# Loading six of eight heads' Wq and Wk in 32-wide blocks, and letting each pair's score weights follow its own product

## The chip, the cores and the metric

The kernel runs on one NeuronCore of a Trainium2 chip. The core has a matrix engine (TensorE, PE in the profile, with its weight loads listed as PEld), a vector engine (VectorE, DVE), an activation engine (ScalarE, ACT), a general engine (GpSimd, POOL) and a queue engine (SyncE, SP) that here issues all the DMAs. Sixteen DMA engines carry the transfers. Each engine works through its own list of instructions in order and waits on semaphores for the others. The metric is device time in microseconds (us), the median of several executions.

## The reference, cut to what matters

Cross attention with a layer norm: 16 batches, 256 query rows of 256 numbers, 77 context rows of 192 numbers, 8 heads of 256. All is float32.

```
Q = x @ Wq            # x (16, 256, 256), Wq (256, 8*256)
K = c @ Wk            # c (16, 77, 192),  Wk (192, 8*256)
V = c @ Wv            # Wv (192, 8*256)
score = Q K^T / 16, per head;  score = -inf where mask == 0
attn  = softmax(score)
out   = concat_heads(attn V) @ Wo + x          # Wo (8*256, 256)
y     = (out - mean) * rsqrt(var + 1e-5) * gamma + beta
```

## The kernel before, in words

The kernel never forms Q, K or V. Per head h it forms G_h = Wk_h Wq_h^T / 16, a matrix of 192 x 256, and U_h = Wv_h Wo_h, once for all batches. A batch's scores are then x (G_h^T c^T), and its output is attn (c U_h). In the code G is split by its 192 rows: `gA` holds the first 128 rows for 8 heads, `gB` the last 64, two heads above each other. `cA` and `cB` hold the transposed context in the same two parts. `prepare_a` (L183) multiplies G with the context of four batches (308 columns): its `part_A` issues the products with gA and cA, four 32-column matmuls beside each other in the array (L202), its `part_B` those with gB and cB, eight beside each other (L216). The results, named a, are what a query tile is multiplied with in `scores` (L319).

The matmuls run in float32; each appears in the trace as two records of weight load and matmul.

Before the loop over batches stands a preparation, about the first 54 us, which the change touches. In order of TensorE's list (L812 to L881):

- `keep_busy` (L657): transposes of the identity whose result is not used, 14 before the first weights and 4 more after the first k transposes.
- `turn_k`, `turn_q`, `turn_k_last`: Wq and Wk need their columns on the partitions for the product G. Heads 0, 1, 4 and 5 are loaded by rows (`wq_nat`, `wk_nat`, `wk_last`) and turned by TensorE, 128 x 128 at a time, into PSUM; ACT and DVE copy the results to `qT` and `kT`.
- `g_of(e)` (L777): G's first 128 rows for two of those heads, scaled by ACT into gA. `rest_of_g(u)` (L791): the last 64 rows, scaled by DVE into gB. Between them `turn_c` turns the first context rows.
- `turn_blk(e)` (L698): heads 2, 3, 6 and 7 are loaded in pieces of 32 rows by 32 columns laid so (`wk_blk`, `wq_blk`) that a DVE transposition of 32 x 32 blocks finishes the turn, into `kT_blk` and `qT_blk`. In this form a pair of heads lies on the two halves of the partitions, and a matmul contracts over 64 rows, two at once in the array.
- `a_of_places((0, 1))`: part_A and part_B for the four turned heads, eight PSUM banks; the copies out alternate between ACT and DVE (`evacuate`).
- `of_pair` (L735) and `rest_of_pairs` (L747): G of the four other heads, then `a_of_places((2, 3))` for them.
- `turn_v` (L727, DVE), then `pu` and `pw`: U of all heads by the same two functions, with Wv and Wo; `turn_rest` turns the remaining context rows on DVE.
- The mask: one 616 KB load broadcasts it to all partitions; DVE turns zeros into large negative numbers (L856) and reduces to find not-a-number entries (L867), POOL folds these in (L868 to L870).
- `transpose_x`: DVE finishes the turn of x for four batches (eight tiles of 128 rows). `prepare_last` (`pr`, L278 and L290) is a product with U for the last 13 context rows of every batch. L290 reads uB, of which half is written by copies on POOL (L865).

Then the loop: for each batch, scores on TensorE, `shift` on DVE, exponentials on ACT, `weigh` on DVE and POOL, `turn` on DVE, and the product with the values. Most batches take `seven`, seven block products in place of eight, fed by sums (`sums`, `differences`) that POOL forms.

The order on each engine is that of the program text; nothing reorders it. SP issues DMAs in order and keeps at most eight in flight: each issue waits until the DMA eight places before it has landed. PSUM is a ring of eight banks under one tag. Tiles of one tag in a pool share a buffer: before, the second half of Wo (`wo_of[1]`) shares that of wq_nat.

Of the kernel before, what the change touches and what calls it, by code (L numbers as in the profile page):

```python
# [15 lines left out]
P = 128  # L16
# [6 lines left out]

# [3 lines left out]
def kernel(  # L54
# [126 lines left out]


    def prepare_a(g, places, B_first=False):  # L183


        if 0 in places:
            a_of[g] = in_two("a", [P, 2, GB, H, S2], g)
        parts = [
            (u + NF * i, dc) for u in places for dc in range(2) for i in range(2)
        ]  # L190
        batches = slice(g * GB, (g + 1) * GB)
        banks = []

        def cols(dc, i):
            return slice((2 * i + dc) * BK, (2 * i + dc + 1) * BK)

        def part_A():
            if not B_first:
                banks.extend(ring_of(parts))
            for (h, dc), o in zip(parts, banks):  # L200
                for i in range(NM):
                    nc.tensor.matmul(  # L202
                        flat(o[i * BK : (i + 1) * BK]),
                        gA[:, h, cols(dc, i)],
                        flat(cA[:, batches, :]),
                        start=not B_first,
                        stop=B_first,
                    )

        def part_B():  # L210
            if B_first:
                banks.extend(ring_of(parts))
            for j in range(0, len(parts), 2):
                for i in range(NM):
                    for k, (h, dc) in enumerate(parts[j : j + 2]):
                        nc.tensor.matmul(  # L216
                            flat(banks[j + k][i * BK : (i + 1) * BK]),
                            gB[half(k), h % NF, cols(dc, i)],
                            flat(cB[half(k), batches, :]),
                            start=B_first,  # L220
                            stop=not B_first,
                        )

        def ring_of(parts):
            return [
                ps_mm.tile([P, GB, S2], F32, tag="mm", name=f"pa_{g}_{h}_{dc}") for h, dc in parts
            ]

        def copies():
            return [(a_of[g][:, dc, :, h, :], o) for (h, dc), o in zip(parts, banks)]  # L230

        return part_A, part_B, copies
# [347 lines left out]

    early = ctx.enter_context(tc.tile_pool(name="early", bufs=1))
    pools[0] = turned = early
    with tc.tile_pool(name="wonce", bufs=1) as wp:
# [4 lines left out]
        wq_nat = wp.tile([P, 2, 2, 2 * D], F32, tag="w128", name="wq_nat")  # L588
        wk_nat = wp.tile([P, 2, 2 * D], F32, tag="wk", name="wk_nat")
        wk_last = wp.tile([P, 2 * D], F32, tag="wl", name="wk_last")  # L590


        wq_blk = wp.tile([P, 2, DI // BK, P], F32, tag="wqb", name="wq_blk")
        wk_blk = wp.tile([P, 2, NL, P], F32, tag="wkb", name="wk_blk")
        wq_blocks = wq.rearrange("(m r) (a i f) -> a i r m f", r=BK, a=NF, i=NM)
        wk_blocks = wk.rearrange("(m r) (a i f) -> a i r m f", r=BK, a=NF, i=NM)
        wq_rows = wq.rearrange("(t p) (e f) -> e p t f", p=P, e=2)
        wk_rows = wk[:P].rearrange("p (e f) -> e p f", e=2)
        wk_ends = wk[P:].rearrange("r (e f) -> (r e) f", e=2)
# [26 lines left out]
        nc.sync.dma_start(wk_nat[:, 0], wk_rows[0][:, : 2 * D])  # L626
        nc.sync.dma_start(wq_nat[:, 0], wq_rows[0][:, :, : 2 * D])
        nc.sync.dma_start(wk_nat[:, 1], wk_rows[1][:, : 2 * D])
        nc.sync.dma_start(wq_nat[:, 1], wq_rows[1][:, :, : 2 * D])
        nc.sync.dma_start(wk_last, wk_ends[:, : 2 * D])  # L630
        nc.sync.dma_start(c_sb, c_rows[:, :first, :])
        for e in range(2):
            load_blocks(wk_blk[:, e], wk_blocks[2 * e + 1])
            load_blocks(wq_blk[:, e], wq_blocks[2 * e + 1])
# [5 lines left out]
            wp.tile([P, 2, 4, DI], F32, tag=tag, name=f"wo_{i}") for i, tag in enumerate(("wo", "w128"))  # L640
# [5 lines left out]
        for a in range(NF):  # L646
            nc.sync.dma_start(wo_of[a // 2][:, a % 2], wo_rows[a])
        load_rest()
        nc.sync.dma_start(
            bias_f.bitcast(I32), mask.rearrange("b k -> (b k)").partition_broadcast(P)  # L650
        )
        load_xT(0)
# [8 lines left out]
        keep_busy(14)  # L661


        qT = const.tile([P, 2, 2, 2, DI], F32, tag="xg0", name="qT")
        kT = const.tile([P, 2, 2, 2, DL], F32, tag="xg2", name="kT")
        qT_blk = const.tile([P, 2, 4, DI], F32, tag="xg1", name="qT_blk")
        kT_blk = const.tile([P, 2, 4, DL], F32, tag="xg3", name="kT_blk")

        def turn_chunks(of, name):

            pt = ps_mm.tile([P, 4, P], F32, tag="mm", name=f"pt_{name}")
            for i, chunk in enumerate(of):
                nc.tensor.transpose(pt[:, i], chunk, ident)
            return pt

        def turn_q(e, u):
            chunks = [
                wq_nat[:, e, t, u * D + dc * P : u * D + (dc + 1) * P]
                for dc in range(2) for t in range(2)
            ]  # L680
            pt = turn_chunks(chunks, f"q_{e}_{u}")
            evacuate(flat(qT[:, e, u]), flat(pt))

        def turn_k(e):
            pt = turn_chunks([wk_nat[:, e, n * P : (n + 1) * P] for n in range(4)], f"k_{e}")
            evacuate(
                kT[:, e].rearrange("p u n l -> p (u n) l")[:, :, :P], pt
            )

        def turn_k_last():  # L690
            pt = turn_chunks([wk_last[:, n * P : (n + 1) * P] for n in range(4)], "kl")
            for e in range(2):
                evacuate(
                    kT[:, e].rearrange("p u n l -> p (u n) l")[:, :, P:],
                    pt.rearrange("p n (r e) -> p e n r", e=2)[:, e],
                )

        def turn_blk(e):  # L698
            for blk, of in ((wk_blk, kT_blk), (wq_blk, qT_blk)):
                nc.vector.transpose(  # L700
                    of[:, e].rearrange("p n (m r) -> p m n r", r=BK),
                    blk[:, e].rearrange("p m (n c) -> p m n c", c=BK),
# [29 lines left out]

# [32 lines left out]
        def wq_part(a, e, n):  # L765
            return qT_blk[half(e), a, n]

        def wk_part(a, e, n):
            return kT_blk[half(e), a, n]

# [6 lines left out]
        def g_of(e):  # L777

            pg = ps_mm.tile([P, 2, DI], F32, tag="mm", name=f"pg_{e}")
            for u in range(2):  # L780
                for dc in range(2):
                    nc.tensor.matmul(  # L782
                        pg[:, u],
                        kT[:, e, u, dc, :P],
                        qT[:, e, u, dc],
                        start=(dc == 0),
                        stop=(dc == 1),
                    )
            nc.scalar.mul(gA[:, NF * e : NF * e + 2], pg, D ** -0.5)

        def rest_of_g(u):  # L791

            ph = ps_mm.tile([P, DI], F32, tag="mm", name=f"ph_{u}")
            for dc in range(2):
                for e in range(2):
                    nc.tensor.matmul(
                        ph[half(e)],
                        kT[:, e, u, dc, P:],
                        qT[:, e, u, dc],
# [3 lines left out]
            nc.vector.tensor_scalar(gB[:, u], ph, D ** -0.5, None, ALU.mult)  # L803

        def a_of_places(places):
            part_A, part_B, copies = prepare_a(0, places)
            part_A()
            part_B()
            for dst, src in copies():
                evacuate(dst, src)  # L810

        turn_k(0)  # L812
        keep_busy(4)
        turn_q(0, 0)
        turn_q(0, 1)
        g_of(0)
        turn_k(1)
        turn_q(1, 0)
        turn_q(1, 1)
# [3 lines left out]
        rest_of_g(0)  # L823
        rest_of_g(1)
        turn_blk(0)
        turn_blk(1)
        a_of_places((0, 1))
        pg = two_banks("pgb", 0)
        for e in range(2):
            of_pair(pg, e, wk_part, wq_part)  # L830
        for i in range(2):
            nc.scalar.mul(gA.rearrange("p (e u) d -> p u e d", e=2)[:, 2 + i], pg[i], D ** -0.5)
        for i, ph in enumerate(rest_of_pairs(0, (0, 1), wk_part, wq_part, "phb")):
            nc.vector.tensor_scalar(gB[:, 2 + i, :], ph, D ** -0.5, None, ALU.mult)
        for a in range(3):
            turn_v(a)
# [3 lines left out]
        a_of_places((2, 3))  # L840
# [15 lines left out]
        nc.vector.tensor_scalar(bias_f, bias_f.bitcast(I32), 0.0, -MASKED, ALU.is_equal, ALU.mult)  # L856
# [9 lines left out]
        nan = wp.tile([P, B, 1], F32, tag="nan", name="nan")  # L866
        nc.vector.tensor_reduce(nan[:, :, 0], bias, AX.X, ALU.max)  # L867
        nc.gpsimd.tensor_tensor(nan, nan, nan, ALU.mult)  # L868
        nc.gpsimd.tensor_tensor(nan, nan, nan, ALU.subtract)
        nc.gpsimd.tensor_tensor(bias, bias, nan.to_broadcast([P, B, S2]), ALU.add)  # L870
# [5 lines left out]
        for j in range(0, GT, 2):  # L876
# [9 lines left out]


# [4 lines left out]
    for b in range(-1, B - 1):  # L892
# [29 lines left out]
        if old and b < B - 2:  # L922
            spread(old[0], old[-1] + 1)
        for _, _, copies in work:
# [100 lines left out]
```

## Time and profile before

| what | value |
|---|---|
| time, median of 3 runs (lowest, highest) | 276.06 us (275.85, 276.31) |
| span of the profiled execution, first to last instruction | 274.2 us |
| the runs' median less that span | 1.9 us |
| TensorE busy (records) | 267.6 us (6012) |
| DVE, POOL, ACT busy | 210.1, 161.0, 132.3 us |
| HBM read and written | 17.57 MB and 4.19 MB |
| first matmul on loaded Wq (pt_q) | at 6.46 us |
| pu begins | at 34.5 us |
| L290 begins | at 48.2 us |
| scores of batch 0 begin | at 54.3 us |
| seven products of batch 0 begin | at 74.6 us |

The profile is of one execution on the chip. It gives no other time for that execution than its span; what a run's time holds beyond the span is taken from the medians. Busy time counts an engine's instructions, but a busy TensorE need not be at its peak, as the ends of matmuls are modelled. The chain is followed back from the last instruction, at each step to what released it, so it tells which engine's time would shorten the run. A wait in brackets behind a group names what ended the idle time before it.

### The profile page before, as it was taken

To read this page: it belongs to the slowest core of one execution; us is meant where nothing else is said; L and a number is where in the kernel's file an instruction comes from. 1 tells how busy PE (TensorE), PEld (TensorE's weight loads), DVE (VectorE), ACT (ScalarE), POOL (GpSimd) and SP (SyncE) were. 2 spreads that over 40 slices of the span, in tenths; PEclk is the share of its full clock that TensorE was granted. 3 is DMA by queue.
4 is the path that set the end of the run, shared out by engine and by line. 5 is a ranking of instruction groups with operands and counts; after the bars stand their busy time and mean duration, and the time that the engine had idled before them with its cause. 6 is when DMAs were issued, how large, how long until landed. Compare 5 with 4: busy or idle time off the path is not lost.

```text
span 274.2 us, 13451 instructions
## 1 busy us (share of the span) xinstructions
PE 267.6 (98%) x6012; PEld 190.4 (69%) x6012; DVE 210.1 (77%) x407; ACT 132.3 (48%) x420; POOL 161.0 (59%) x222
## 2 busy tenths in 40 slices
PE   7999999999999999999999999999999999999993
PEld 7857486777494949595958586867777776584652
DVE  0364966697749898979789797878788978889875
ACT  2314112354818282737464646455464644727652
POOL 1000004939677878787868777777787537255754
PEclk9999999999999999999999999999999999999998
DMA  6996999920000131410230405000505060110102
GB/s 179 245 204 167 338 148 175 239 41 5 4 4 2 57 65 44 154 45 4 59 63 22 100 14 182 28 18 10 116 5 117 2 196 2 41 41 4 60 23 79
DMA packets 40458, 22.63 MB, mean 83 GB/s; under 512 B 23424, under 2 KB 38864, under 8 KB 40400
## 3 DMA queue, kind: packets, MB, share of 16 engines
q1 hardware_dynamic: 40400, 21.77, 32.0%
q8 instruction: 47, 0.77, 1.3%
q14 instruction: 11, 0.09, 0.1%
HBM read 17.57 MB, written 4.19 MB: 79 GB/s over the span
## 4 chain that ended last, share of the span: by engine, by line
PE 96%; DMA 2%; DVE 1%; issue 0%; SPq 0%; DVEq 0%
PE ps L319 25%; PE pa L202 12%; PE pv L244 10%; PE po L452 9%; PE pm L452 8%; PE po L384 7%; PE pa L216 6%; PE pv L255 6%; PE pu L739 3%; PE pr L278 2%; DMA wq_nat<-in_L_xattn_Wq_dram 2%; PE pg L782 1%; PE pgb L739 1%; PE pw L753 1%; PE pr L290 1%; PE po L400 1%
## 5 line engine op out<-in xcount | busy, mean ns | idle before, releaser
L348 ACT ACTIVATE e<-s,top 128x77 f32<-128x77 f32 x256 | 67.1, 346 | 68.0 <-DVE top L341 65.4
L362 POOL TENSOR_TENSOR p<-e,rden 128x512 f32<-128x512 f32 x64 | 47.3, 760 | 42.3 <-DVE rden L356 29.8
L319 PE MATMUL ps<-a,xT 128*32 128x154 f32 x2048 | 70.0, 294 | 0.0
L319 PEld LDWEIGHTS ps<-a,xT 128*32 128x32 f32 x2048 | 66.1, 110 | 1.7 <-issue 0.8
L334 DVE TENSOR_TENSOR s<-ps,bias 128x308 f32<-128x308 f32 x64 | 30.3, 475 | 17.7 <-PE ps L319 17.6
L202 PE MATMUL pa<-cA,gA 128*32 128x308 f32 x512 | 35.8, 423 | 0.0
L202 PEld LDWEIGHTS pa<-cA,gA 128*32 128x32 f32 x512 | 16.4, 110 | 20.9 <-issue 8.0
L485 POOL TENSOR_TENSOR xg<-xg,m 128x256 f32<-128x256 f32 x33 | 24.1, 731 | 11.4 <-DVE xg L499 9.6
L244 PE MATMUL pv<-uA,cA 128*32 128x512 f32 x256 | 30.4, 592 | 0.0
L354 DVE TENSOR_REDUCE den<-e 128x8 f32<-128x616 f32 x32 | 24.7, 773 | 4.4 <-ACT e L348 4.4
L372 DVE STREAM_TRANSPOSE pT<-p 128x640 f32<-128x640 f32 x32 | 25.4, 816 | 1.8 <-POOL p L362 1.8
L341 DVE TENSOR_REDUCE top<-s 128x8 f32<-128x616 f32 x32 | 25.4, 795 | 1.1
L926 ACT COPY vw<-pv 128x512 f32<-128x512 f32 x32 | 17.1, 586 | 8.8 <-PE pv L255 8.8
L415 POOL TENSOR_TENSOR ts<-vw 128x768 f32<-128x768 f32 x11 | 20.3, 1843 | 0.0
L568 DVE SCALAR_TENSOR_TENSOR xg<-xg,rstd,bet 128x256 f32<-128x256 f32 x24 | 18.7, 780 | 1.8
L216 PE MATMUL pa<-cB,gB 64*32 64x308 f32 x512 | 19.5, 420 | 0.0
L216 PEld LDWEIGHTS pa<-cB,gB 64*32 64x32 f32 x512 | 9.7, 107 | 11.3 <-issue 7.6
L255 PE MATMUL pv<-uB,cB 64*32 64x512 f32 x256 | 17.4, 601 | 0.0
L384 PE MATMUL po<-vw,pT 128*32 128x256 f32 x288 | 17.3, 380 | 0.0
L926 ACT COPY a<-pa 128x308 f32<-128x308 f32 x48 | 16.8, 455 | 0.0
L499 DVE TENSOR_TENSOR xg<-po,xg 128x256 f32<-128x256 f32 x31 | 11.7, 412 | 6.1 <-PE po L452 5.6
L452 PE MATMUL po<-vr,pT 128*32 128x128 f32 x352 | 15.7, 273 | 0.0
(121 smaller groups left out, 386.3 us busy)
## 6 DMA issues: line engine op xcount, KB each, us to landing
xg<-in_x_dram SPq DMA_DIRECT2D x4, 1024.0 KB, 6.3
xT<-in_x_dram SPq DMA_DIRECT2D x24, 128.0 KB, 3.5
out_dram<-xg SPq DMA_DIRECT2D x11, 256.0 KB, 2.5
wo<-in_L_xattn_Wo_dram SPq DMA_DIRECT2D x4, 512.0 KB, 5.1
wvT<-in_L_xattn_Wv_dram SPq DMA_DIRECT2D x16, 96.0 KB, 3.4
out_dram<-xg SPq DMA_DIRECT2D x10, 128.0 KB, 1.7
wq_nat<-in_L_xattn_Wq_dram SPq DMA_DIRECT2D x2, 512.0 KB, 6.3
wq_blk<-in_L_xattn_Wq_dram SPq DMA_DIRECT2D x8, 128.0 KB, 5.2
```

The costliest lines, as they stand in the source:

```text
L202: nc.tensor.matmul(flat(o[i * BK : (i + 1) * BK]), gA[:, h, cols(dc, i)], flat(cA[:, batches, :]), start=not B_first, stop=B_first,)
L216: nc.tensor.matmul(flat(banks[j + k][i * BK : (i + 1) * BK]), gB[half(k), h % NF, cols(dc, i)], flat(cB[half(k), batches, :]), start=B_fir ...
L244: nc.tensor.matmul(pv[k][i * BK : (i + 1) * BK], cA[:, b, k * BK : (k + 1) * BK], uA[:, parts, :, i], start=True, stop=False,)
L255: nc.tensor.matmul(pv[k][i * BK : (i + 1) * BK], cB[half(k), b, k * BK : (k + 1) * BK], uB[half(k), parts, :, i], start=False, stop=True,)
L319: nc.tensor.matmul(ps[m // 2][i * BK : (i + 1) * BK, m % 2 * 2 * S2 : (m % 2 + 1) * 2 * S2], xT_of[g][:, j * NM + m, dc], flat(a_of[g][:, ...
L334: nc.vector.tensor_tensor(s[:, a * H // 2 : (a + 1) * H // 2], ps[a][:, : H // 2 * S2].rearrange("p (h k) -> p h k", k=S2), bias[:, b, :]. ...
L341: nc.vector.tensor_reduce(top, s, AX.X, ALU.max, negate=True)
L348: nc.scalar.activation(e[:, h], s[:, h], AF.Exp, bias=top[:, h : h + 1])
L362: nc.gpsimd.tensor_tensor(part, e_mh[:, :, :, keys], rden_mh.unsqueeze(3).to_broadcast(list(part.shape)), ALU.mult,)
L384: nc.tensor.matmul(po[i * BK : (i + 1) * BK], pT[:, n, i], vw_of[b][:, 2 - n // 2 * 2 : 4 - n // 2 * 2, n % 2, :] if n < NF else vr[:, b, ...
L452: nc.tensor.matmul(out[i * BK : (i + 1) * BK], weight[:, i], moving, start=(n == 0), stop=(n == len(terms) - 1),)
L926: nc.scalar.copy(dst, src)
```

## The change

- Only heads 0 and 1 are loaded by rows and turned by TensorE: 14 transposes in place of 28. `wq_nat` comes in two loads of 256 KB, one per head, `wk_last` in two of 64 KB. Each head's q copies are split between DVE and ACT.
- Heads 2 to 7 are loaded in blocks, as three pairs; a pair's `turn_blk` runs one pair ahead.
- After each pair's G (`g_of_pair`, `rest_of_g_of_pair`) its part_A and part_B follow at once (`a_of_pair`), on four banks, with all four copies on ACT. Pairs are now heads 2a and 2a + 1. In `rest_of_g_of_pair` the product is cut into two halves of 128 columns, so that each half of the banks holds one, and DVE writes gB in four pieces.
- `keep_busy` has 12 transposes at the start and none later.
- The mask is loaded and prepared in two parts, batches 0 to 3 and 4 to 15 (`load_bias`, `bias_of`); the second part's work on DVE and POOL moves into the first pass of the loop, behind the weighing. x for the first four batches is loaded in two halves; the second half's DVE turns move to the same place.
- `wo_of[1]` now shares the buffer of wq_blk.

```diff
@@ loads
-        wq_blk = wp.tile([P, 2, DI // BK, P], F32, tag="wqb", name="wq_blk")
-        wk_blk = wp.tile([P, 2, NL, P], F32, tag="wkb", name="wk_blk")
+        wq_blk = wp.tile([P, NF - 1, DI // BK, P], F32, tag="wqb", name="wq_blk")
+        wk_blk = wp.tile([P, NF - 1, NL, P], F32, tag="wkb", name="wk_blk")
...
-        nc.sync.dma_start(wk_nat[:, 0], wk_rows[0][:, : 2 * D])
-        nc.sync.dma_start(wq_nat[:, 0], wq_rows[0][:, :, : 2 * D])
-        nc.sync.dma_start(wk_nat[:, 1], wk_rows[1][:, : 2 * D])
-        nc.sync.dma_start(wq_nat[:, 1], wq_rows[1][:, :, : 2 * D])
-        nc.sync.dma_start(wk_last, wk_ends[:, : 2 * D])
+        nc.sync.dma_start(wk_nat, wk[:P, : 2 * D])
+        for e in range(2):
+            nc.sync.dma_start(wq_nat[:, :, e * D : (e + 1) * D], wq_rows[:, :, e * D : (e + 1) * D])
+        for e in range(2):
+            nc.sync.dma_start(wk_last[half(e)], wk_ends[:, e])
         nc.sync.dma_start(c_sb, c_rows[:, :first, :])
-        for e in range(2):
-            load_blocks(wk_blk[:, e], wk_blocks[2 * e + 1])
-            load_blocks(wq_blk[:, e], wq_blocks[2 * e + 1])
+        for a in range(1, NF):
+            load_blocks(wk_blk[:, a - 1], wk_blocks[a])
+            load_blocks(wq_blk[:, a - 1], wq_blocks[a])
...
-            wp.tile([P, 2, 4, DI], F32, tag=tag, name=f"wo_{i}") for i, tag in enumerate(("wo", "w128"))
+            wp.tile([P, 2, 4, DI], F32, tag=tag, name=f"wo_{i}") for i, tag in enumerate(("wo", "wqb"))
...
-        nc.sync.dma_start(
-            bias_f.bitcast(I32), mask.rearrange("b k -> (b k)").partition_broadcast(P)
-        )
-        load_xT(0)
+        load_bias(0, GB)
+        load_xT(0, 0, GT // 2)
+        load_xT(0, GT // 2, GT)
+        load_bias(GB, B)
...
-        keep_busy(14)
+        keep_busy(12)
@@ the products
+        def turn_q(e):
+            for dc, copy in enumerate((nc.vector.tensor_copy, nc.scalar.copy)):
+                pt = ps_mm.tile([P, 2, P], F32, tag="mm", name=f"pt_q_{e}_{dc}")
+                for t in range(2):
+                    nc.tensor.transpose(
+                        pt[:, t], wq_nat[:, t, e * D + dc * P : e * D + (dc + 1) * P], ident
+                    )
+                copy(qT[:, e, dc], flat(pt))
...
+        def g_of_pair(a):
+            banks = [ps_mm.tile([P, DI], F32, tag="mm", name=f"pgb_{a}_{e}") for e in range(2)]
+            for n in range(4):
+                for e in range(2):
+                    nc.tensor.matmul(
+                        banks[e],
+                        kT_blk[a][half(e), n, :P],
+                        qT_blk[a][half(e), n],
...
+            for e, o in enumerate(banks):
+                nc.scalar.mul(gA[:, 2 * a + e], o, D ** -0.5)
+
+        def rest_of_g_of_pair(a):
+            banks = [ps_mm.tile([P, P], F32, tag="mm", name=f"phb_{a}_{e}") for e in range(2)]
+            for n in range(4):
+                for i in range(2):
+                    for e in range(2):
+                        nc.tensor.matmul(
+                            banks[e][half(i)],
+                            kT_blk[a][half(e), n, P:],
+                            qT_blk[a][half(e), n, i * P : (i + 1) * P],
...
+            for e, o in enumerate(banks):
+                for i in range(2):
+                    nc.vector.tensor_scalar(
+                        gB[half(e), a, i * P : (i + 1) * P], o[half(i)], D ** -0.5, None, ALU.mult
+                    )
+
+        def a_of_pair(a):
+            part_A, part_B, copies = prepare_a(0, (a,))
+            part_A()
+            part_B()
+            for dst, src in copies():
+                nc.scalar.copy(dst, src)
@@ their order
-        turn_k(0)
-        keep_busy(4)
-        turn_q(0, 0)
-        turn_q(0, 1)
-        g_of(0)
-        turn_k(1)
-        turn_q(1, 0)
-        turn_q(1, 1)
-        turn_k_last()
-        g_of(1)
-        turn_c()
-        rest_of_g(0)
-        rest_of_g(1)
-        turn_blk(0)
-        turn_blk(1)
-        a_of_places((0, 1))
...
-        a_of_places((2, 3))
+        turn_k()
+        turn_q(0)
+        g_of(0)
+        turn_q(1)
+        turn_k_last()
+        g_of(1)
+        turn_c()
+        rest_of_g()
+        turn_blk(1)
+        a_of_pair(0)
+        for a in range(1, NF):
+            g_of_pair(a)
+            rest_of_g_of_pair(a)
+            if a + 1 < NF:
+                turn_blk(a + 1)
+            else:
+                for i in range(3):
+                    turn_v(i)
+            a_of_pair(a)
@@ the mask and x
+    def bias_of(lo, hi):
+        part = bias[:, lo:hi]
+        part_f = bias_f[:, lo * S2 : hi * S2]
+        nc.vector.tensor_scalar(part_f, part_f.bitcast(I32), 0.0, -MASKED, ALU.is_equal, ALU.mult)
+        nan = st.tile([P, hi - lo, 1], F32, tag="nan", name=f"nan_{lo}", bufs=1)
+        nc.vector.tensor_reduce(nan[:, :, 0], part, AX.X, ALU.max)
+        nc.gpsimd.tensor_tensor(nan, nan, nan, ALU.mult)
+        nc.gpsimd.tensor_tensor(nan, nan, nan, ALU.subtract)
+        nc.gpsimd.tensor_tensor(part, part, nan.to_broadcast([P, hi - lo, S2]), ALU.add)
...
-        nc.vector.tensor_scalar(bias_f, bias_f.bitcast(I32), 0.0, -MASKED, ALU.is_equal, ALU.mult)
+        bias_of(0, GB)
...
-        nan = wp.tile([P, B, 1], F32, tag="nan", name="nan")
-        nc.vector.tensor_reduce(nan[:, :, 0], bias, AX.X, ALU.max)
-        nc.gpsimd.tensor_tensor(nan, nan, nan, ALU.mult)
-        nc.gpsimd.tensor_tensor(nan, nan, nan, ALU.subtract)
-        nc.gpsimd.tensor_tensor(bias, bias, nan.to_broadcast([P, B, S2]), ALU.add)
...
-        for j in range(0, GT, 2):
+        for j in range(0, GT // 2, 2):
             transpose_x(0, j)
@@ the loop over batches, behind exponential and weigh
+        if b < 0:
+            bias_of(GB, B)
+            for j in range(GT // 2, GT, 2):
+                transpose_x(0, j)
```

## The prediction

> **What bounds the kernel now.** I read the page first (busy time, then the chain by engine), then the chain in order of time, then the timeline of the first 56 us, where the change lies. The page:
>
> ```profile
> span 274.2 us, 13451 instructions
> ...
> PE 267.6 (98%) x6012; PEld 190.4 (69%) x6012; DVE 210.1 (77%) x407; ACT 132.3 (48%) x420; POOL 161.0 (59%) x222
> ...
> PE 96%; DMA 2%; DVE 1%; issue 0%; SPq 0%; DVEq 0%
> ```
>
> TensorE (PE) holds 96% of the chain, so another engine matters only where it makes PE wait. The chain in order of time (start, length, what):
>
> ```profile
> 1.16 5.25 DMA wq_nat<-in_L_xattn_Wq_dram
> ...
> 7.99 1.97 PE pg L782 x8
> ...
> 14.08 1.88 PE ph L796 x16
> 15.96 4.28 PE pa L202 x64
> 20.24 2.23 PE pa L216 x64
> 22.48 3.65 PE pgb L739 x32
> 26.13 1.89 PE phb L753 x32
> ...
> 34.53 7.11 PE pu L739 x64
> ```
>
> The only long item besides PE is the first wq_nat load, landing at 6.41. From there PE runs almost gapless to pu at 34.5 and on to the end: a DMA's arrival, then a sum of PE blocks. On the timeline two later waits come close to PE:
>
> ```profile
> 44.73 0.80 DVE L856 TENSOR_SCALAR bias<-bias 128x1232 f32<-128x1232 int32 x1 [2.32 <-DMA bias<-in_mask_BxS_if_dram]
> ...
> 48.15 2.83 PEld L290 LDWEIGHTS pr<-cRB,uB 64*64 64x64 f32 x64 [0.30 <-POOL uB L865]
> ```
>
> DVE is stopped 2.3 us by the mask; its uB copies queue behind that, POOL's uB copies behind those, and PE at L290 is released by POOL, still without a hole in the chain.
>
> **What the Trainium skill says.** "TensorE: Matmul & The Clock Gate", section "What's actually happening": PE's clock starts at half rate and goes full after about 3.4 us of sustained activity. The trace agrees: 14 idle transposes from 1.36 take 3.25 us (0.21 each at steady rate), eight at 6.46 take 1.10 (0.11 each). "TensorEngine Tiling (Array Packing)", "Key Properties": changing the tiling mode drains the array. The trace agrees: each block here costs 0.14 to 0.19 us beyond its streaming (below).
>
> **The change, part by part.** Times are of the profiled execution, against its 274.2 us span; the runs' median is 276.06, 1.9 us lie around the span, and I carry that over.
>
> Start. wk_nat (256 KB) lands 3.1 us after issue, at 3.84; the 512 KB wq_nat at 6.41, 2.6 us later. The new first wq_nat is 256 KB in pieces of 1 KB instead of 2: half of 2.6 is 1.3, 1.6 if short pieces cost more. It lands at 5.15 to 5.45; I take 5.35, a gain of 1.1 us. PE itself is free at about 4.8 (12 idle and 4 k transposes at 0.21).
>
> Early blocks. Transposes of q, k and kl fall from 28 to 14; the 14 removed are 14 x 0.11 = 1.5 us less PE. From 5.35: four q transposes, still at the slow clock (0.9), their halves copied by DVE and ACT side by side (0.42, from the 128x256 copy of kT), so g_of(0) starts at 6.7. It is half of L782's x8, so 0.9; then 6 transposes 0.7; a wait of 0.3 for the qT halves; g_of(1) 0.9; turn_c 0.6 as before; rest_of_g half of L796 plus switch, 1.0. A of pair 0 starts at 11.2; before, pa started at 15.96 after twice the heads.
>
> Longer or shorter blocks. Each matmul leaves two records. Four pa matmuls run beside each other, one such group per 0.26 us, and 16 groups make 4.14 of L202's 4.28; the rest, 0.14, is the block's own start. The same split: L216 8 x 0.26 + 0.16; pgb 16 x 0.216 + 0.19; phb 8 x 0.216 + 0.16. A pair now has four blocks: g_of_pair 8 x 0.216 + 0.19 = 1.92; rest_of_g_of_pair 16 matmuls of 128 columns, four at once, 8 groups; A 8 x 0.26 + 0.14 = 2.2; B 4 x 0.26 + 0.16 = 1.2. The 64x64 weight with 128 columns has no row. The nearest, pm L452 with 128 columns, has 64 records in 1.89 us, 0.11 per group of four without starts: 0.88 + 0.16 = 1.03. From below it can't go under that stream time, 0.88; from above, if weight loads of 0.13 each limited it, 8 x 0.13 + 0.16 = 1.2. I take 1.03. So a pair is 6.4 us, three are 19.1, pair 0's A and B are 3.4: pu starts at 11.2 + 3.4 + 19.1 = 33.7, against 34.5. Arithmetic is unchanged; 1.5 us of transposes are saved and about 1.3 us returned, since the A, B and G blocks number 14 instead of 6, at 0.16 each.
>
> Does DVE keep up? Per pair it does four gB evictions of 64x128 behind phb (no row: 0.2 each as half of L834's 0.42 at 128x256, up to 0.42; I take 0.23), then turn_blk of the next pair, 0.95 + 1.22 (L700). With hand-overs 3.3 us, while PE needs 3.4 for that pair's A and B. It just hides; at 0.42 each PE would stand 0.7 us at each of two pairs. ACT has four a copies (0.52 apart) and two gA (0.37 each), 2.8 us of 6.4: hidden.
>
> Do the loads keep up? Bytes ahead of wv are the same. In before the second half's blocks landed by 21.2 (DVE L700 waited 2.0 for them), a pair's 896 KB of blocks in 4.2 to 5.2 us. Natural rows now end near 8, so pair 1 lands at 12.3 to 13.0, pair 2 near 17, pair 3 near 22. They are wanted at 13.2 (the qT turn must start then for PE at 14.6), 19.7 and 26. Pair 1 is the tight one, up to 0.5 us. On SP the eight more block issues keep the pace of the landings they wait for. The wo rows of pairs 2 and 3 now share wq_blk's buffer and wait for turn_blk(3), near 27.3; before, they were issued from 27.6. No loss, unless pair 3 slips; behind them on SP stand the context, the mask and x.
>
> pu to prepare_last. The turns of wv (1.6 each, three then one) start at 31.3 and end at 37.6, each before its pu block. PE reaches L290 at 47.4. Its releaser changes: the mask for four batches is a quarter of 616 KB and no longer the late item; now it is cB's last block of context rows. That landed at 40.5; then turn 1.1, uA copy 0.7, bias_of's two DVE steps (0.25 + 0.4, from 0.80 and 1.44 at four times the width), POOL's nan steps and sum (0.3 + 0.3 + 0.6), which now stand ahead of the uB copies, and six of those at 0.46. PE is released at 47.2, if the context lands no later than before. It hides by 0.2. The half of turned x (512 KB instead of 1 MB ahead of scores) lands near 46, wanted at 53: hidden. The split costs SP five more issues (one mask, four x, about 0.45 each, 2.3 us) ahead of load_x(0), gamma and beta; those rows landed at 53 to 55 and are first read by the batch 0 sums near 78: hidden by more than 20 us.
>
> Moved into the first pass: bias_of(4, 16) and two x turns put 0.6 + 1.1 + 1.3 us on DVE after the weighing and 2.3 on POOL before differences. Behind them turn(0), turn(1) and the next shift come 2.1 to 2.5 us later, and sums end 18.1 us after that pass's scores began. seven(0) on PE starts 20.3 after (74.6 against 54.25). Hidden by 2.2 us; without that cover the price would be the excess.
>
> Sum: 1.1 (earlier start) less 0.3 in the early blocks is 0.8, and 0.1 from L290's small release delay that goes: 274.2 - 0.9 = 273.3 span, 275.2 for the runs.
>
> **The rivals.** (1) The gain is lost to the loads at L290 or the pairs: no change. For it: the block loads move in 512 byte pieces, DMA is 0.9 to 1.2 busy in most slices from 2 to 20 us, and three DVE and POOL steps now lie between the context and PE. If the context lands d later, PE gets 1.1 - d; with d of 0.6 to 1.6 the result lies within 0.5 of before. I take d = 0.9: 275.9. Against: the same bytes lead, and SP's issue, not DMA, was the limit from 22 to 26 (busy share 0.4 to 0.6).
> (2) More gain. If the first wq_nat lands at 4.8, where PE is free, and loads and DVE never bite, another 0.5 to 0.7: 274.5. For it: of the 16 DMA engines the first had delivered its share of the 512 KB at 4.45, only the last at 6.41.
> (3) Slower: PE's clock. The second keep_busy (four transposes) is gone, and PE stands idle from 4.8 until wq_nat lands. If that hole, with the one before g_of(0), spoils the activity window that made the clock full near 6.2, one more window of 3.4 us passes at half rate, 1.7 us of lost work: 275.2 + 1.7 = 276.9. It decides from a hole of unknown length; the forecast's is 0.5 us in 3.4. Against: the window stays some 80% busy.
> That the change doesn't do what it says I hold unlikely: the orders of the engines show the blocks where the diff puts them.
>
> **How the numbers follow.** Forecast 275.2 with chance 0.50 (own range 274.8 to 275.5: start time and a few tenths at pair 1); rival 1 0.25; rival 2 0.10; rival 3 0.15. 0.2% is 0.55 us, about what a measurement of this kernel can tell from no change, so faster means below 275.5. That is nearly all of the forecast and rival 2, 0.58; same is most of rival 1 and the forecast's edge, 0.27; slower is rival 3, 0.15. The range from 274.5 to 276.6 holds the forecast, rival 1, the near half of rival 2 and the edge of rival 3; it takes in DVE at 0.42 per eviction (+1.4) and the weight loads (+0.5).
>
> **What would show it.** Start: pt_q released by wq_nat near 5.3. Clock: eight-transpose spacing 0.11 by g_of(0). Blocks: phb 128 columns at 1.0 per pair, pa A 2.2, B 1.2. DVE: no PE wait named L685 at the second and third pair. pu at 33.7. L290's successor released by POOL near 47.4. If pu starts early but scores do not, rival 1 holds; if the early blocks themselves are long, rival 3. The forecast is wrong if PE waits for a turn_blk by more than 0.3 per pair, or if the seven-product block of batch 0 waits for sums.

## The result and the profile after

After: 276.63 us, median of 21 runs; before, beside it on the same chip: 276.13 us. The ratio is 1.0015 with a 95% interval of 1.0003 to 1.0027. Measured again beside each other (below) the two kernels gave 276.46 against 275.89 us, 1.0021 (1.0008 to 1.0035). So the change costs about half a microsecond, where I had forecast a gain of 0.9: the time came out 1.4 us above the forecast of 275.2 and just past the upper end of its range, 276.6. The profiled execution has a span of 274.8 us, 0.6 us above that of before.

Where the front gained is seen on TensorE's timeline of after (start and length in us, engine and line, operation, out<-in, matmul tile, shapes, count of records; in brackets an idle time and what ended it):

```profile
4.91 0.70 PE L664 MATMUL pt_q<-ident,wq_nat 128*128 128x128 f32 x4
...
13.89 2.00 PE L783 MATMUL pgb<-qT,kT 64*128 64x256 f32 x16
15.82 1.10 PE L799 MATMUL phb<-qT,kT 64*64 64x128 f32 x32
...
20.42 2.00 PE L783 MATMUL pgb<-qT,kT 64*128 64x256 f32 x16
...
33.31 7.18 PE L723 MATMUL pu<-wo,wv_turned 64*128 64x256 f32 x64
...
46.99 0.57 PE L260 MATMUL pr<-cRB,uB 64*64 64x208 f32 x4
```

The first transposes of Wq start at 4.91 us instead of 6.46, the product of Wv and Wo (pu) at 33.31 instead of 34.47, and `pr`'s second part (L260, L290 of before) at 46.99 instead of 48.15: 1.16 us gained, more than the 0.8 forecast, and still in hand at 47 us. The next step takes it away. The chain of waits for this stretch, in order of time (start, length, what), first before's, then after's:

```profile
41.64 3.61 PE pw L753 x64
45.26 2.96 PE pr L278 x32
48.22 3.14 PE pr L290 x62
51.36 2.96 PE pr L278 x32
54.32 1.69 PE ps L319 x45
```

```profile
31.61 4.21 SPq L593
35.86 1.06 SPq L593
36.97 1.49 SPq L593
38.50 3.19 DMA cB<-in_ctx_dram
41.79 1.11 DVE cB L601
42.93 0.69 DVE uA L123
43.65 0.48 DVE bias L555
44.16 0.48 DVE nan L557
...
45.28 0.71 POOL bias L560
46.04 0.39 POOL uB L865
...
48.32 0.41 POOL uB L865
48.77 3.03 PE pr L260 x60
51.80 2.96 PE pr L248 x32
54.77 4.32 PE ps L289 x128
```

In before, this stretch of the chain was TensorE alone. Now it comes through the landing of the context's last block (41.69 us; 40.48 in before), goes over VectorE's (DVE) turn and one copy of uA, the two DVE steps of the mask, POOL's three steps of the mask and six of POOL's eight copies of uB, and reaches TensorE at 48.77. Four records of L260 went ahead at 46.99; the other 60 take 3.03 us, as long as the whole block takes without a wait (3.04 in the first experiment), so the block is 48.77 - 46.99 = 1.78 us late. The scores start at 54.70 us instead of 54.25. Ahead of the landing the chain is SyncE itself, issuing the context's loads (SPq L593): one issue takes 4.21 us, with six loads in flight at its start and three at its end, fewer than the eight that the kernel allows. Before has such a long issue too (3.81 us at 29.68); what holds SyncE there no run shows.

From there on the work of the two kernels runs alike: in the traces of both kernels and of all variants below, each of the 16 batches' scores starts within 0.01 us of the same distance from the first (199.42 or 199.43 us from the first to the last), seven(0) starts 20.34 us after the scores in both, and DVE's last instruction ends 217.4 us after them in both. So the work moved into the loop's first pass is hidden.

One difference is left at the very end. From the landing of the last output to the end of the span 0.84 us pass in before and 1.03 us in after. SyncE's list closes with one wait on a semaphore in before and with four in after, some 0.06 us each. Every kernel of this document with mask and x in one piece takes 0.83 to 0.85 us there, every one with the split 1.00 to 1.10. So of the 0.64 us between the two spans, 0.45 are the later scores and 0.19 this closing, for which my prediction had nothing.

### The profile page after: what moved, and what is told of

It reads as the page before. It is cut to its first block, busy times and chain, and to the rows that moved or that the text cites. A ratio compares the mean times of both kernels' runs of the same rounds, so it can differ in the third digit from the quotient of the medians.

```text
span 274.8 us, 13574 instructions
## 1 busy us (share of the span) xinstructions
PE 266.8 (97%) x6056; PEld 188.2 (68%) x6056; DVE 210.5 (77%) x411; ACT 134.0 (49%) x431; POOL 161.9 (59%) x225
## 4 chain that ended last, share of the span: by engine, by line
PE 81%; SPq 8%; DMA 6%; DVE 2%; POOL 1%; issue 1%; DVEq 0%; POOLq 0%
PE ps L289 24%; PE pv L214 10%; PE pa L172 9%; PE po L422 9%; PE pm L422 8%; PE po L354 7%; PE pv L225 6%; DMA wq_blk<-in_L_xattn_Wq_dram 5%; PE pa L186 5%; SPq L593 3%; SPq L582 3%; DMA cB<-in_ctx_dram 1%; PE pr L260 1%; PE pr L248 1%; POOL uB L865 1%
## 5 line engine op out<-in xcount | busy, mean ns | idle before, releaser
L385 POOL TENSOR_TENSOR ts<-vw 128x768 f32<-128x768 f32 x11 | 20.2, 1838 | 0.0
```

## The experiments

**Theories.** In the trace of after two things stand between TensorE and its uB: the context's landing, 1.2 us later than in before (D), and the mask's steps, put ahead of the uB copies on DVE and POOL (P). As my prediction had it, either alone would leave the wait hidden or nearly so; so the question is which of them carries it. "Theory J" below is that both are needed, "theory M" that the split mask's steps alone are what costs.

**The mask's steps behind the copies.**

```diff
-        bias_of(0, GB)
         for j in range(NF // 2):
...
+        bias_of(0, GB)
         for u in (uA, uB):
```

> Theory P (the gain is lost in POOL's queue: the mask's steps stand ahead of the eight copies of uB): the copies can start when cRB is copied, at 44.4 us in the trace of after, and eight of them at 0.45 us end at 48.0 instead of 48.7; the second half of the sixteen-batch product's remainder starts 0.7 us earlier, and so does all that follows: 0.5 to 0.8 us below after, about 0.3 us below before. Theory D (the gain is lost only because the context's remainder lands 1.2 us later): VectorE and POOL still start from the same landing at 41.7 us, and the time stays that of after within 0.2 us.

275.45 us, ratio to before 0.9981 (0.9969 to 0.9993): 1.0 to 1.2 us below after's two medians. POOL and TensorE on this kernel's timeline:

```profile
43.23 0.36 POOL L603 COPY cRB<-cB 128x208 f32<-128x208 f32 x1
43.65 3.67 POOL L864 COPY uB<-uB 64x256 f32<-64x256 f32 x8
```

```profile
47.02 3.04 PE L260 MATMUL pr<-cRB,uB 64*64 64x208 f32 x64
49.99 3.03 PE L248 MATMUL pr<-cRA,uA 128*64 128x208 f32 x32
```

The copies follow the context's own copies at once, L260 runs through, the scores start at 52.95. P is right in kind; its size was too small because it waited for all eight copies, where six are enough. The context landed at 40.84 us here, 0.85 earlier than in the first trace of after, so the medians and the pair below are the better measure. D alone falls.

**After again, and the mask's addition twice.** Both measured beside each other:

```diff
-        nc.gpsimd.tensor_tensor(part, part, nan.to_broadcast([P, hi - lo, S2]), ALU.add)
+        for _ in range(2 if lo == 0 else 1):
+            nc.gpsimd.tensor_tensor(part, part, nan.to_broadcast([P, hi - lo, S2]), ALU.add)
```

> The kernel after, unchanged, as a second look beside the runs of this comparison. Theory J: the context lands between 41 and 42 us again, at least 0.5 us later than the 40.1 to 40.5 of the kernel before, the remainder waits 0.9 to 1.4 us for POOL, and the time is 0.2 to 0.6 us above before. Rival X (the late landing was an accident of one execution): the context lands by 40.6, no wait, 0.9 us below before.

> After, with POOL's addition of the first four batches' mask made twice, 0.7 us more ahead of the copies of uB. Theory P/J: POOL is what the remainder waits for, and the wait grows by the whole 0.7 us: 0.6 to 0.8 us above after. Theory D alone (the wait is for the context): POOL has room, less than 0.2 us above after.

After again: 276.46 us. With the addition twice: 277.41 us, ratio to before 1.0062 (1.0036 to 1.0088), 0.95 us above after and a little more than expected. The timelines, after again first, then the doubled addition:

```profile
44.51 0.70 POOL L560 TENSOR_TENSOR bias<-bias,nan 128x308 f32<-128x308 f32 x1
45.27 3.58 POOL L865 COPY uB<-uB 64x256 f32<-64x256 f32 x8
```

```profile
47.07 0.57 PE L260 MATMUL pr<-cRB,uB 64*64 64x208 f32 x4
47.99 3.03 PE L260 MATMUL pr<-cRB,uB 64*64 64x208 f32 x60 [0.36 <-POOL uB L865]
```

```profile
44.68 1.47 POOL L561 TENSOR_TENSOR bias<-bias,nan 128x308 f32<-128x308 f32 x2
46.22 3.57 POOL L866 COPY uB<-uB 64x256 f32<-64x256 f32 x8
```

```profile
47.26 0.57 PE L260 MATMUL pr<-cRB,uB 64*64 64x208 f32 x4
48.93 3.03 PE L260 MATMUL pr<-cRB,uB 64*64 64x208 f32 x60 [1.10 <-POOL uB L866]
```

The context landed at 40.93 us in both (in the trace of after above it was 41.69), and L260 is 0.92 and 1.67 us late: 0.75 more for 0.77 more of addition. POOL is what TensorE waits for, one for one. After again and the kernel with the steps behind are the cleanest pair: the context's last copy on POOL (cRB) begins at 43.24 and 43.23 us, the uB copies at 45.27 and 43.65, the scores at 53.92 and 52.95; the medians differ by 1.01 us. The expectation of a landing after 41 us missed: it came at 40.93, and L260 still waited. Between the two traces of after the landing differs by 0.76 us and the start of the scores by 0.78: the landing, too, passes through one for one.

**Earlier context, by leaving a load out.** The last quarter of Wo is not loaded; heads 6 and 7 take the rows of heads 4 and 5. Once as after, once with the mask's steps behind.

```diff
-        for a in range(NF):
+        for a in range(NF - 1):
             nc.sync.dma_start(wo_of[a // 2][:, a % 2], wo_rows[a])
...
         def wo_part(a, e, n):
+            a = min(a, NF - 2)
             return wo_of[a // 2][half(e), a % 2, n, :]
```

> The last quarter of Wo isn't loaded; heads 6 and 7 use the rows of heads 4 and 5, so this quarter's share of the result is left out. All loads behind it move up by what it took, about 1.3 us. Theory D: the context lands at about 40.4 us, VectorE's turning, POOL's copies and the remainder's start move up by the same 1.2 us, and the time is 1.0 to 1.3 us below after. Theory P: the mask's steps still stand ahead of the copies; VectorE's bias steps end at 43.4, POOL's at 44.7, eight copies of 0.45 us end at 48.3: only 0.3 to 0.5 us below after.

> As in the run before, the last quarter of Wo is left out; and the mask's steps stand behind the copies of uB. Theory P with D as its second half: POOL is free at 43.2 us, eight copies end at 46.8, just before TensorE wants them (46.99): no wait is left and the time is 1.6 to 1.8 us below after. Theory D alone: the same 1.0 to 1.3 us as with the quarter left out and the mask's steps where they are.

275.75 us, 0.9998 (0.9983 to 1.0012), and 275.22 us, 0.9975 (0.9966 to 0.9984). In the first, the context landed at 40.17 us, the sixth copy of uB ended at 47.19 and L260 ran without a stop from 47.48, with the mask's steps where they were. But pair 1's blocks came late there (TensorE stood 0.37 us for their turn, pu began at 33.79): at after's 46.99 L260 would still have waited 0.2 us. The time lies between the two expectations. With both, 0.2 us less than with the steps behind alone, within the intervals: 1.2 to 1.4 us below after, less than P had given it (1.6 to 1.8) and about what D had (1.0 to 1.3).

What these runs show is P, with D adding to it; J is not shown. In three traces with the mask's steps ahead (both of after and this one) the sixth copy ended 7.01 or 7.02 us after the landing. At before's landings, 40.10 to 41.07 us in three traces, that would be 47.1 to 48.1, still later than the 46.99 at which L260 was reached (an estimate from these figures). An earlier landing so makes the wait smaller; putting the steps behind took it away.

**POOL's copies halved.** All of Wo again, the steps behind, and ScalarE (ACT) writes its half of uB to both places.

```diff
                     engine(here, pw[half(i)].rearrange("p (n c) -> p n c", c=BK))
-                    nc.gpsimd.tensor_copy(there, here)
+                    if i:
+                        nc.gpsimd.tensor_copy(there, here)
+                    else:
+                        engine(there, pw[half(i)].rearrange("p (n c) -> p n c", c=BK))
```

> All of Wo is loaded again. The mask's steps stand behind the copies of uB, and ScalarE writes its halves of uB to both places out of PSUM, so that POOL has four copies instead of eight. Theory P: POOL's four end at about 46.2 us, VectorE's at 45.1, ScalarE's at about 45.5 (0.31 us each); the remainder's wait goes and the time is 1.6 to 1.8 us below after, about 274.8 us where before has 276.1. Theory D alone: the context lands as late as in after, so the time stays within 0.3 us of after.

> The kernel before, with nothing else than ScalarE writing its halves of uB to both places. Theory J: before waits only 0.17 us at the remainder, so it gains 0.0 to 0.2 us; what the repaired kernel gains over before is then the change's own. Rival R (the repair is worth the same to both kernels): 0.7 to 1.0 us below before.

275.13 us, 0.997 (0.996 to 0.998), with the context as late as in after (41.65 us) and no wait at L260: 1.3 to 1.5 us below after's two medians, short of the 1.6 expected at least. The same copies in the kernel before: 275.94 us, 0.9994 (0.9981 to 1.0008), nothing measurable. Nor could the order of the mask's steps give before much: its whole wait at L290 is 0.17 us (3.21 us for the block instead of 3.04). So what the repaired kernel gains is the new front's own.

**The mask and x whole again.** After's front, `load_bias(0, B)` and `load_xT(0)` in one piece, the mask's steps as in before.

> After's front, with the mask and the turned x loaded and worked on as before (mask whole, VectorE's comparison ahead of its uB copies, the rest of the mask's steps behind all of uB). Theory J (the wait needs both the later context and the mask's steps ahead of POOL's copies, and the split of the mask is what spares the wait for the whole mask): the mask of 616 KB lands about 45.9 us, VectorE's uB copies start at 46.7, POOL's sixth copy ends at 49.2: the remainder's wait is 0.5 us longer than in after and the time 0.3 to 0.6 us above after. Theory M (the split mask's steps are what costs, the front alone would have gained): no mask step stands on POOL ahead of the copies, the time is 0.5 to 1.0 us below after, the same as with the steps behind.

> After's front with the mask and the turned x whole, unchanged, beside after itself. Theory J: with the context at 41.7 us the whole mask lands at about 45.2 us, VectorE's copies start at 46.0, POOL's sixth ends at 48.5: the same place as in after, the time within 0.3 us of after. Theory M: 0.5 us or more below after.

> The mask and x whole as in the run before, but all of the mask's steps behind the copies of uB, and ScalarE writing its halves twice. If the split of the mask and x is worth nothing by itself (theory Z): the wait goes, the scores start at about 53.2 us and the time is that of the run with the split mask repaired in the same way, 1.2 to 1.5 us below after. Rival Y (x in one piece is late for scores that start at 53.2): x lands at 51.5 to 52.9 us, its first turning ends 0.7 us later, the scores wait up to 0.5 us, and the time is 0.7 to 1.1 us below after.

275.82 and 275.86 us (0.9994, 0.9978 to 1.001; 1.0, 0.998 to 1.0021): the front alone neither gains nor loses. That is 0.6 us below after, measured beside it, nearer to M than to J; 0.19 us of it is the shorter closing. The two profiled executions were slower than that: the whole mask landed at 45.86 and 45.25 us, DVE's copies stood behind it and L260's later records began at 49.47 and 49.01, later than in after; those executions took 277.1 and 276.65 us, well above their kernels' medians. They seem to have caught late landings: the same list of loads landed the mask at 44.70 and 43.50 us in the traces of the two other kernels with the whole mask, below. L260's later records followed the mask's landing by 3.61 and 3.76 us; by that, a landing near 44.5 us would give the medians (an estimate). The front's gain then went into the wait for the mask that before already had (DVE stood until 44.73). With all mask steps behind the copies and ACT's double writing, but mask and x whole (the third run), 274.85 us, 0.9958 (0.9943 to 0.9973): as good as the split mask repaired in the same way, whose 275.13 us hold 0.19 us more of closing. Splitting mask and x bought nothing that an order on POOL and DVE doesn't buy; x landed at 52.06 and TensorE didn't wait for it.

**DVE between the pairs.** gB's four evictions per pair from DVE to ACT, on the repaired kernel with the split mask and on that with the whole mask.

```diff
-                    nc.vector.tensor_scalar(
-                        gB[half(e), a, i * P : (i + 1) * P], o[half(i)], D ** -0.5, None, ALU.mult
-                    )
+                    nc.scalar.mul(
+                        gB[half(e), a, i * P : (i + 1) * P], o[half(i)], D ** -0.5
+                    )
```

> The run with ScalarE's copies of uB and the mask's steps behind, and gB's four small evictions of each pair moved from VectorE to ScalarE, which idles from 16.6 to 19.9 us. Theory V (VectorE's 1.25 + 0.98 + 1.20 us between a pair's remainder and the next pair's G sets the cadence): pairs 2 and 3 start 0.15 us earlier each, the product of Wv and Wo 0.3 us earlier, and the time is 0.2 to 0.3 us below that run. Rival W (the blocks' landing sets it): the same within 0.1 us.

> Mask and x whole, all mask steps behind the copies of uB, ScalarE writing its halves twice, and gB's small evictions on ScalarE. Theory V: pairs 2 and 3 start 0.15 us earlier each; 0.2 to 0.3 us below the same kernel without the last step, about 274.6 us where before has 276.0. Rival Y: x lands at about 52 us, its first turning ends at 52.7, just ahead of scores that would start at 52.9 to 53.2; in some executions they wait and the gain is under 0.1 us.

275.0 us, 0.9966 (0.9954 to 0.9979), and 274.45 us, 0.9955 (0.9937 to 0.9973), the lowest of all, against 0.997 and 0.9958 without: the times don't tell them apart. The traces do: pairs follow each other by 6.37 us (G of pair 1 at 14.37, of pair 2 at 20.74) where in after it is 6.53, 0.16 each at two pairs.

**Why the context lands late.** Pair 3's columns of Wk and Wq by rows (packets of 1 and 2 KB) instead of blocks (512 bytes), then those of all three pairs (the edit shown); the same bytes in the wrong order, so G of heads 6 and 7, or 2 to 7, is not computed rightly. And before once more.

```diff
-            load_blocks(wk_blk[:, a - 1], wk_blocks[a])
-            load_blocks(wq_blk[:, a - 1], wq_blocks[a])
+            nc.sync.dma_start(to_k[:, : 2 * D], wk[:P, a * 2 * D : (a + 1) * 2 * D])
...
+            for t in range(2):
+                nc.sync.dma_start(to_q[:, t], wq[t * P : (t + 1) * P, a * 2 * D : (a + 1) * 2 * D])
```

> After, with pair 3's columns of Wk and Wq loaded in rows of 1 and 2 KB (5 DMAs) in place of blocks of 512 bytes (8 DMAs), the same bytes; they land in the wrong order, so G of heads 6 and 7 is not computed rightly. Theory L (the third pair's small blocks are what makes the loads late): Wv's last block lands about 1 us earlier, the context by 41.0 us or before, and the remainder's wait shrinks to 0.4 us or less: 0.7 to 1.2 us below after. Rival N (the lateness isn't the blocks'): the context lands at 41.4 to 41.8 and the time is that of after within 0.2 us.

> The run with pair 3 alone by rows, again (G of heads 6 and 7 is not computed rightly). Theory L: the context between 40.3 and 41.1 us, a time between those of after and of the run with all pairs by rows. Rival N: 40.9 to 42, as in after.

> After, with the columns of Wk and Wq of pairs 1, 2 and 3 loaded by rows of 1 and 2 KB (15 DMAs) in place of blocks of 512 bytes (24 DMAs), the same bytes; they land in the wrong order, so G of heads 2 to 7 is not computed rightly. Theory L (the 512-byte packets, about 41 ns each where a packet of 2 KB took about 100, are what fills the queue): Wv's last block lands by 28 us, the context by 40.0 us, the wait goes, and the time is 0.9 to 1.3 us below after. Rival N (the queue's backlog isn't the blocks'): the context lands at 40.9 to 41.7 us and the wait stays.

> The kernel before, a second look at its landings: Wv's last block at 28.5 to 28.6 us and the context at 40.0 to 40.5 us, if before's loads are as steady as its two looks show; anything from 41 on would take the lateness from the change.

Pair 3 alone: 276.1 us (1.0003, 0.9992 to 1.0015) and 276.02 us (0.9994, 0.9976 to 1.0012), the context at 41.10 and 41.60 us, L260 still waiting: no help at the landing, and a time between those of after and of the run with all three. All three: 275.07 us, 0.9969 (0.996 to 0.9979), Wv's last block at 25.86 us instead of 30.03, the context at 38.00, no wait, and a gain of 1.4 to 1.6 us on after's two medians, above the expected 0.9 to 1.3. What the queue moved in the first 30 us (40 slices of 0.75 us), before, after, and all by rows:

```profile
GB/s 0 0 117 295 330 221 180 227 227 364 365 284 237 173 191 208 189 213 220 210 212 217 244 203 189 148 195 173 204 186 208 143 21 174 199 167 240 214 328 322
```

```profile
GB/s 0 0 147 262 317 339 201 266 215 171 225 206 208 199 208 197 213 210 220 191 202 159 176 199 200 170 262 224 159 187 112 182 196 149 261 181 189 198 235 308
```

```profile
GB/s 0 0 142 306 284 331 194 217 291 220 245 251 352 356 251 220 363 374 268 205 341 216 208 203 207 141 168 148 275 197 117 36 229 183 279 393 415 148 202 202
```

Where blocks are loaded the queue moves some 200 GB/s, where rows are, up to 365 or 374. The packets' own times say the same: those of 512 to 2048 bytes up to 32 us sum, over 16 engines, to 22.7 to 23.5 us in three traces of before's loads, 24.5 to 26.9 in ten of after's, 25.3 and 25.5 with pair 3 by rows, and 20.2 with all by rows. The Trainium skill, "DMA: Bandwidth & Descriptors", section "Why small descriptors are slow (HBM only)", gives a fixed cost of about three cycles per packet beside one per 32 bytes; by that, a 512-byte packet would lose some 16% (an estimate: 3 of 19 cycles). The trace agrees in sign and shows more: 41 ns per 512-byte packet in after, against 109 ns per 2 KB in before, 164 against 109 for the same bytes. So blocks make the loads slower; shown for three pairs, not for one, where the 2 KB packets took 127 to 134 ns each. And one pair is what the change itself moved from rows to blocks: with pair 3 by rows there are as many 512-byte packets as in before (6656), and the context still came at 41.10 and 41.60. The run with all rows also has fewer and larger loads (15 instead of 24), so that eight in flight can hold more bytes; packet length and load size were not told apart.

The landing isn't steady either: 40.74 to 42.90 us, mean 41.50, in ten traces of after's loads, and 40.48, 40.10 and 41.07, mean 40.55, in three of before's. The last (before again, a single execution of 276.4 us) missed its expectation: it lies past the 41 us that I had set as the sign against the change, and inside after's range; there the front was 0.6 us later too (pu at 35.04). So the context comes about 1 us later in after on the mean, but the two ranges overlap.

## Why the prediction was wrong

- **Start.** Larger than forecast: the first half of Wq landed at 4.65 us (5.35 forecast, 4.8 in rival 2), pt_q ran at 4.91.
- **Clock (rival 3).** Refuted: the four transposes of turn_q(1) took 0.60 us, as four of before's did at 9.79.
- **Blocks.** Right: phb of 128 columns 15.82 to 16.85, 1.03 us as forecast, with no limit by weight loads; A 2.22 and B 1.19 (2.2 and 1.2).
- **DVE "just hides".** Short by 0.16 us per pair: a 64x128 eviction took 0.31 us (four in 1.25), not 0.23, and PE's weight loads at pairs 2 and 3 are named as waiting for L685. It cost 0.3 us in all.
- **Loads at pair 1.** Called tight, and were: landed at 12.30 in after with no loss, but in three other kernels with the same loads up to there TensorE stood 0.37, 0.58 and 0.74 us.
- **Loop and load_x.** Right: nothing seen of them. The closing of the span, 0.19 us longer, stood in no sum.
- **"PE is released at 47.2, if the context lands no later than before. It hides by 0.2."** This step failed, in three terms. The condition did not hold: 41.50 us on the mean instead of 40.5. I had taken "Bytes ahead of wv are the same" for the same time, though two pairs by blocks had become three (896 KB each); that this one pair made the difference is not shown. From landing to release 7.02 us passed (41.69 to 48.72, and 40.93 to 47.94 in the second trace of after) where I had 6.7, of which the steps that I listed make only 6.4; DVE's two mask steps took 0.48 each (0.25 and 0.4 forecast, by dividing a wider row by four; the small steps don't shrink so far). And L260 was reached at 47.0, not 47.4, because the start gained more. With these, it hides only if the context lands by 40.0, which no trace of after's loads showed, nor one of before's: the wait would have come with the context on time, only shorter.
- **Rival 1** named the place and the reason; its price, "1.1 - d", left out that what stands ahead of the copies had grown as well, so that it ended at no change instead of a loss. The release is an absolute time: landing plus 7.02 us. It was 48.3 us in before, set by the mask, and 48.7 in after, so that an earlier arrival at it brings nothing.

What stays open: what makes the context land about 1 us later, as one pair by rows does not bring it forward (its packets' sum is hardly less, but what makes them long was not tried), and what holds SyncE in its long issues.

## What to carry to other kernels

A front that gets faster only carries its gain as far as the first join with something that didn't: work out that release from the landing that feeds it, with the landing's spread over executions, not from one trace and a margin of 0.2 us. Work that nobody waits for soon (here the mask's steps) belongs behind the copies that someone waits for, on every in-order queue it passes; that order alone was worth 1.0 us here, and with half the copies on another engine too, landings as late as 41.65 and 42.00 us left no wait. And equal bytes need not be equal time: count a load's packets and their length before and after.

## What was not expected of the hardware

Blocks of 512 bytes moved at some 200 GB/s and rows of 1 to 2 KB at up to 374, on the same queue with eight transfers in flight. One and the same list of loads landed its last context block anywhere between 40.74 and 42.90 us, while the scores of TensorE's loop behind it repeated to 0.01 us. The end of the program had a price as well: three more waits of SyncE's were 0.19 us. And in after TensorE's transposes went from one per 0.213 us to one per 0.109 at 5.12 us, before the first product at 6.00: what the prediction reads as the clock going full came on transposes alone.
